# Handing a block's repeated dt x input to the drives when it is loaded

## The chip, the cores and the metric

The kernel runs on one core of one Trainium2 chip. The core has five engines that work side by side, each through its own queue and strictly in the order of that queue: PE (matrix products), DVE (vector), ACT (activations), POOL (a second, slower vector engine) and SP, which here only issues DMAs. The metric is device time of one execution in microseconds, as the median of several runs: 3704.53 us before the change (three runs, 3703.52 to 3707.54).

## The reference

Two layers on a batch of 8 images with 384 channels and 32 x 32 pixels, all in float32. The first is a state-space (Mamba-like) layer, the second a small mixture of experts; the part that the change touches is the scan of the first:

```python
dt = softplus(dt @ dt_proj_w.T + dt_proj_b)
dA  = exp(einsum('bld,dn->bldn', dt, A))            # "decay"
dBu = einsum('bld,bln->bldn', dt * xc, Bm)          # "drive"
h   = dA_t * h + dBu_t                              # scan over the 1024 tokens
y_t = einsum('bdn,bn->bd', h, C_t)                  # "read" and sum over the 16 states
y   = (y + xc * D) * silu(z)                        # "finish"
t   = gelu((y @ out_proj_w.T) @ mlp_w1.T + b1) @ mlp_w2.T + b2
```

Before it come a group norm, a layer norm, a projection and a short convolution that make xc, z, dt, B and C. After it every expert's `relu(x @ w1 + b1)` is computed for every token, and the four results are weighted by a routing that depends on the whole batch: its second product can only start when all tokens have been scored.

## The kernel before, in words

The 8 x 1024 tokens are cut into 16 chunks of 512 tokens. A chunk has 768 inner channels with 16 states each. These are worked off in **rounds**: 6 blocks of 128 channels, and for each block 4 rounds, so 24 rounds a chunk and 384 in all. One round holds 128 channels x 4 states; a tile row holds one of 32 channels and one of 4 states, and four such tiles make the round: two of pair A, two of pair B. So dt and dt x input must stand in SBUF with each channel repeated on four partitions. `delta` (L464) makes them for a block: it computes dt, multiplies it with the input (POOL, `dtx` L489), writes both to DRAM and reads them back with repetition: `dtr_a` and `dtr_b` (dt for the decays of pair A and B) and `dxr` (dt x input, four loads of 256 KB). `dxr` and `dtr_b` have two buffers, `dtr_a` has one.

A round then goes through the engines like this:

- ACT: four decays (L854), two of pair A and two of pair B, into three PSUM buffers.
- POOL: the **drive** (L866), one multiplication of `dxr` by the row of B, 128x2048, into one of five `du` buffers. The buffer comes free when PE has summed the round that used it five rounds ago.
- DVE: four scans (L874), and for pair A the read-outs (L878), products with the row of C.
- POOL: the **read** of pair B (L878, 128x1024), after the pair's scans; in the even chunks a carry copy (L883) before it.
- PE: for every two rounds 16 small products (`y`, L901) that sum over the states. They wait for the reads of both rounds.
- After a block's last sum DVE multiplies with z (`finish`, L911). When all six blocks of a chunk are finished, PE may start that chunk's out projection (L554), and then its MLP (L576, L618); later the experts' first products (L729) of the chunk.

PE, ACT and DVE do the chunk's projections, norms and MLP between the rounds. The order in every queue is written by a planner that is part of the kernel and runs when it is built. It holds a clock of its own for PE, DVE, ACT and POOL, with a fixed duration for each kind of step, and at each moment issues on a free engine the due step of the earliest round, or a side task that fits before the next one. Two of its chains matter here, both on POOL: `pool_a` holds the 384 drives and `pool_b` the 384 reads. A drive is due when the planner has issued the sums that free its buffer and when `dxr` of its block is on the planner's list. If a drive and a read are due at once, the one of the earlier round goes first. What is issued goes into the engine's queue in that order; the real waits are set by semaphores on the data.

A block's `dxr` gets onto that list in `delta`, in this passage (L519 to L529):

```python
        x4 = pdt.tile([P, Q, T], F32, name="dxr")
        for j in range(Q):
            repeat(x4[:, j, :], there_x, j)
            yield "-", PIECE / 2 if i + d else 0
        while issued["A"] < last:
            yield "-", POLL
        dxr[i, d] = x4
```

`last` is the last round of the block before. `issued["A"]` is the last round whose pair A decays the planner has put into ACT's queue. So the planner lets no drive of a block go before the last pair A decay of the block before it is issued. That wait is needed for `dtr_a`, which has a single buffer and is loaded in the lines that follow; `dxr` has a second one.

After the scans (some 3022 us in) PE does the last chunk's out projection and MLP, the routing is worked out, the experts' remaining first products follow, and then only the experts' second products (L1235). Half of chunk 13's expert products and all of the last two chunks' are held back by the kernel until the last chunk is summed.

Of the kernel before, what the change touches and what calls it, by code (L numbers as in the profile page):

```python
# [49 lines left out]
DMA = 3.5  # L50
# [27 lines left out]
def build(tc, io):  # L78
# [3 lines left out]
    with ExitStack() as outer:  # L82
# [47 lines left out]
        with ExitStack() as ctx:  # L130
            layers(ctx, tc, io, ident, cmean, eps, dram, x1_dram, gn1, logits, r_dram, group_norm)


def layers(ctx, tc, io, ident, cmean, eps, dram, x1_dram, gn1, logits, r_dram, group_norm):
# [83 lines left out]
    xc, zs, dtr, dxr, dbc, bc_dram, bt, ct, gn = {}, {}, {}, {}, {}, {}, {}, {}, {}  # L218
# [13 lines left out]
    def bank(name):  # L232
        held[0] += 1
        current[0].holds += 1
        return ps_g.tile([P, T], F32, name=name, tag="g")

    def free():
        held[0] -= 1
        current[0].holds -= 1
# [214 lines left out]
    def written(name, i, d, what):  # L454
        there = dram.tile([P, T], F32, name=f"{name}_dram{i}_{d}")
        nc.sync.dma_start(there, what)
        return there

    def repeat(into, there, j):

        rows = there[j * (P // Q):(j + 1) * (P // Q), :]
        nc.sync.dma_start(into, rows.unsqueeze(1).to_broadcast([P // Q, Q, T]))

    def delta(i, d):  # L464
        while i not in dbc or making_dt:
            yield "-", POLL
        making_dt.append((i, d))
        yield "bank", MM
        g = bank("g_dt")
        PE.matmul(g, lhsT=w_dt[:, d * P:(d + 1) * P], rhs=dbc[i], start=True, stop=True)  # L470
        yield "ACT", EVICT_ROW
        projected.add((i, d))
        dt = p1.tile([P, T], F32, name="dt")
        S.activation(dt, g, AF.Relu, bias=b16[:, d:d + 1], scale=-1.0)
        yield "ACT", 0.7
        S.activation(dt, dt, AF.Exp, bias=top, scale=-1.0)
        yield "ACT", FUNC
        S.activation(dt, dt, AF.Ln, bias=1.0)
        yield "DVE", TAIL
        V.scalar_tensor_tensor(dt, g, b_dt[:, d:d + 1], dt, ALU.add, ALU.max)  # L480
        yield "-", 0
        free()
        there = written("dtr", i, d, dt)
        if i + d == 0:
            yield "DVE", JOIN
        else:
            yield "POOL", MULT
        dtx = p1.tile([P, T], F32, name="dtx")
        (G if i + d else V).tensor_tensor(dtx, dt, xc[i, d], ALU.mult)  # L489
        yield "-", 0  # L490
        there_x = written("dxr", i, d, dtx)
        yield "-", DMA if i + d else 0
        making_dt.clear()
        if i + d == 0:

            b, a = pdt.tile([P, 2, T], F32, name="dtr_b"), p1.tile([P, 2, T], F32, name="dtr_a")
            x4 = pdt.tile([P, Q, T], F32, name="dxr")
            repeat(b[:, 0, :], there, 2)
            for j in (2, 3):
                repeat(x4[:, j, :], there_x, j)  # L500
            repeat(a[:, 0, :], there, 0)
            for j in (0, 1):
                repeat(x4[:, j, :], there_x, j)
            repeat(b[:, 1, :], there, 3)
            repeat(a[:, 1, :], there, 1)
            dtr[i, d], dxr[i, d] = {"A": a, "B": b}, x4
            return
        last = i * per + d * NG - 1
        while issued["B"] < last - NG:
            yield "-", POLL  # L510
        dtr[i, d] = {}
        pair = pdt.tile([P, 2, T], F32, name="dtr_b")
        for k in range(2):
            repeat(pair[:, k, :], there, 2 + k)
        yield "-", 0
        while issued["drive"] < last - NG:
            yield "-", POLL
        dtr[i, d]["B"] = pair
        x4 = pdt.tile([P, Q, T], F32, name="dxr")  # L519
        for j in range(Q):  # L520
            repeat(x4[:, j, :], there_x, j)
            yield "-", PIECE / 2 if i + d else 0
        while issued["A"] < last:
            yield "-", POLL
        dxr[i, d] = x4
        pair = p1.tile([P, 2, T], F32, name="dtr_a")
        for k in range(2):
            repeat(pair[:, k, :], there, k)
        dtr[i, d]["A"] = pair  # L529


    stats = {}
    tt, x1, hs, pre, ready = {}, {}, {}, {}, {}
# [426 lines left out]
    def begin(*new, rank=2, after=None, holds=0):  # L960
        for t in new:
            tasks.append(Task(t, rank, now[0] if after is None else after))
            tasks[-1].holds += holds
# [96 lines left out]
    def plan(i, k):  # L1060

        n = i + 1
        if k % 4 == 1 and k // 4 + 2 < ND:
            begin(delta(i, k // 4 + 2), rank=0)
        if k in (2, 3, 4):
            begin(gate(i, k + 1))
        if k == 4:
            begin(silus(zs, gates, [(i, d) for d in range(3, 6)]))
        if n < NCH:
            if 4 <= k < 10:  # L1070
                begin(conv(n, k - 4), rank=1)
            if k in (6, 9):
                begin(silus(xc, accs, [(n, k - 6 + d) for d in range(3)]), rank=1)
            if k in (11, 12, 13):
                begin(gate(n, k - 11))
            if k == 9:
                begin(x_proj(n), rank=1)
            if k == 13:
                begin(silus(zs, gates, [(n, d) for d in range(3)]))
            if k == 15:  # L1080
                begin(delta(n, 0), rank=0)
            if k == 20:
                begin(delta(n, 1), rank=0)
        if k == 20 and n + 1 < NCH:
            begin(norm(n + 1), rank=1)
        if k == 3 and i + NH < NCH:
            begin(next_x(i))
        if k == 3 and i % NH == 0 and i + NH < NCH:
            begin(statistics(i // NH + 1), rank=3)
# [248 lines left out]
```

## Time and profile before

One execution was profiled: 3700.98 us, with a span of 3699.2 us from the first to the last instruction.

| | |
|---|---|
| median of three runs | 3704.53 us |
| the profiled execution | 3700.98 us |
| its span | 3699.2 us |
| PE busy | 3483.4 us, 94% |
| DVE busy | 3071.8 us, 83% |
| POOL busy | 2771.7 us, 75% |
| ACT busy | 2352.6 us, 64% |
| 383 drives on POOL (L866) | 1737.4 us, 4.542 us each |
| 384 reads on POOL (L878) | 906.4 us, 2.362 us each |
| mean granted PE clock | 0.971 of full speed |

The shares are means over stages that differ. Until some 65 us the first chunk is normalized and projected; then the rounds run, from the first drive at 67 us to the last sum at 3024 us; after that DVE, ACT and POOL have little to do. The tables of busy time by stretches of time, in the next section, show this better than the shares of the whole.

### The profile page before, as it was taken

Reading aid. Unit: us, or ns where it says so; the run is one execution under the profiler, and the core shown is the slowest. Engines: PE = TensorE matmul, PEld = TensorE weight load, DVE = VectorE, ACT = ScalarE, POOL = GpSimd, SP = SyncE. Lnnn points to the kernel's source line nnn. Section 1 sums busy time; section 2 is a strip of 40 time slices with the busy share of each in tenths; the row PEclk is TensorE's granted clock in tenths of the full one; section 3 lists DMA queues with packets and bytes.
Section 4 is the critical chain, followed back from the end, with each engine's and each line's share of the span. In section 5 each row is a group of like instructions: output and inputs, shape, how many; then the busy total and the mean of one; then the engine's idle time right before and its main releaser. Section 6 shows DMA issues by size and latency. Waiting matters only on the chain.

```text
span 3699.2 us, 35905 instructions
## 1 busy us (share of the span) xinstructions
PE 3483.4 (94%) x10342; PEld 1406.0 (38%) x10342; DVE 3071.8 (83%) x3675; ACT 2352.6 (64%) x3714; POOL 2771.7 (75%) x1071
## 2 busy tenths in 40 slices
PE   6759797999999999999999999999999999999999
PEld 3213232334333433333333333333433334444444
DVE  4999999899999999999999999999999861355554
ACT  4758687868787878786978787879687743100000
POOL 2999999899999999999899999998999960000000
PEclk8869898999999999999999999999999999999999
DMA  3434455465656565656565656565655544655552
GB/s 121 152 125 154 157 175 191 161 207 184 201 176 215 187 211 181 201 191 216 176 214 182 215 178 207 191 211 180 211 167 204 187 145 145 228 187 186 187 187 101
DMA packets 387928, 674.81 MB, mean 182 GB/s; under 512 B 42876, under 2 KB 153852, under 8 KB 385556
## 3 DMA queue, kind: packets, MB, share of 16 engines
q1 hardware_dynamic: 385568, 672.18, 54.5%
q8 instruction: 84, 1.38, 0.2%
q14 instruction: 112, 0.92, 0.1%
q10 hardware_dynamic: 2164, 0.34, 0.1%
HBM read 534.33 MB, written 138.02 MB: 182 GB/s over the span
## 4 chain that ended last, share of the span: by engine, by line
PE 56%; DVE 20%; ACT 10%; POOL 5%; DMA 4%; issue 4%; SPq 1%; ACTq 0%; POOLq 0%; DVEq 0%
PE acc L1235 13%; PE g_in L342 9%; PE hid L576 8%; DVE da_A L874 7%; PE e_hid L729 7%; DVE du L874 6%; PE acc L618 6%; PE y L901 5%; PE g_out L554 5%; POOL du L866 3%; DVE du L878 3%; POOL du L878 2%; ACT da_B L854 1%; PE g_dt L470 1%; ACT L222 1%
## 5 line engine op out<-in xcount | busy, mean ns | idle before, releaser
L866 POOL TENSOR_TENSOR du<-dxr,b 128x2048 f32<-128x2048 f32 x383 | 1737.4, 4542 | 0.8 <-DMA b<-bc_dram 0.8
L878 POOL TENSOR_TENSOR du<-du,c 128x1024 f32<-128x1024 f32 x384 | 906.4, 2362 | 109.5 <-DVE du L874 88.6
L854 ACT ACTIVATE da_A<-dtr_a,w_a_log 128x512 f32<-128x512 f32 x768 | 519.8, 686 | 235.4 <-DVE du L878 68.0
L854 ACT ACTIVATE da_B<-dtr_b,w_a_log 128x512 f32<-128x512 f32 x768 | 523.0, 686 | 210.3 <-DVE du L878 73.6
L342 PE MATMUL g_in<-xt,in_proj 128*128 128x512 f32 x1152 | 532.8, 604 | 24.1 <-DMA in_proj<-in_in_proj 13.6
L618 PE MATMUL acc<-h,mlp_w 128*128 128x512 f32 x1152 | 535.3, 604 | 20.8 <-ACT h L592 13.1
L878 DVE TENSOR_TENSOR du<-da_A,c 128x512 f32<-128x512 f32 x768 | 529.4, 689 | 24.0 <-DMA c<-bc_dram 0.2
L576 PE MATMUL hid<-tt,mlp_w 128*128 128x512 f32 x1152 | 520.9, 597 | 6.9 <-DMA mlp_w<-in_mlp_w 1.6
L874 DVE TENSOR_TENSOR_SCAN da_A<-da_A,carry,du 128x512 f32<-128x512 f32 x384 | 490.7, 1278 | 23.0 <-POOL du L866 14.3
L874 DVE TENSOR_TENSOR_SCAN du<-da_B,carry,du 128x512 f32<-128x512 f32 x384 | 475.8, 1269 | 35.4 <-ACT da_B L854 35.0
L1235 PE MATMUL acc<-r,w_e_w 128*128 128x512 f32 x1152 | 494.6, 592 | 0.0
L729 PE MATMUL e_hid<-xn,e_w 128*128 128x512 f32 x1008 | 464.1, 601 | 22.2 <-DMA e_w<-in_e_w 11.3
L874 DVE TENSOR_TENSOR_SCAN da_A<-da_A,du 128x512 f32<-128x512 f32 x384 | 467.3, 1217 | 19.0 <-POOL du L866 12.9
L901 PE MATMUL y<-du,sel 128*32 128x512 f32 x3072 | 413.1, 623 | 69.5 <-POOL du L878 56.7
L874 DVE TENSOR_TENSOR_SCAN du<-da_B,du 128x512 f32<-128x512 f32 x384 | 452.8, 1207 | 26.9 <-ACT da_B L854 25.8
L342 PEld LDWEIGHTS g_in<-xt,in_proj 128*128 128x128 f32 x1152 | 218.6, 193 | 318.7 <-issue 266.4
L618 PEld LDWEIGHTS acc<-h,mlp_w 128*128 128x128 f32 x1152 | 216.7, 192 | 315.1 <-issue 256.9
L576 PEld LDWEIGHTS hid<-tt,mlp_w 128*128 128x128 f32 x1152 | 214.1, 190 | 298.0 <-issue 246.2
L1235 PEld LDWEIGHTS acc<-r,w_e_w 128*128 128x128 f32 x1152 | 218.9, 190 | 275.5 <-issue 275.3
L729 PEld LDWEIGHTS e_hid<-xn,e_w 128*128 128x128 f32 x1008 | 190.0, 192 | 272.0 <-issue 223.3
L554 PE MATMUL g_out<-xc,out_proj 128*128 128x512 f32 x576 | 265.2, 601 | 0.0
L743 ACT ACTIVATE r<-e_hid,w_e_b 128x512 f32<-128x512 f32 x192 | 129.5, 679 | 153.4 <-PE e_hid L729 90.7
(135 smaller groups left out, 3049.0 us busy)
## 6 DMA issues: line engine op xcount, KB each, us to landing
dxr<-dxr_dram SPq DMA_DIRECT2D x384, 256.0 KB, 4.6
mlp_w<-in_mlp_w SPq DMA_DIRECT2D x384, 192.0 KB, 3.6
dtr_b<-dtr_dram SPq DMA_DIRECT2D x192, 256.0 KB, 3.3
dtr_a<-dtr_dram SPq DMA_DIRECT2D x192, 256.0 KB, 3.1
r_dram<-r SPq DMA_DIRECT2D x192, 256.0 KB, 3.8
r<-r_dram SPq DMA_DIRECT2D x64, 768.0 KB, 4.6
in_proj<-in_in_proj SPq DMA_DIRECT2D x192, 192.0 KB, 3.9
e_w<-in_e_w SPq DMA_DIRECT2D x192, 192.0 KB, 4.1
```

The lines of the kernel that those rows point to most:

```text
L342: PE.matmul(g, lhsT=w[:, j, :], rhs=xt[i][:, j, :], start=(j == 0), stop=(j == J - 1))
L554: PE.matmul(g, lhsT=w[:, d, :], rhs=xc[i, 3 * k + d], start=(k + d == 0), stop=(k == 1 and d == 2))
L576: PE.matmul(g, lhsT=w[:, j, :], rhs=tt[i][:, j, :], start=(j == 0), stop=(j == J - 1))
L618: PE.matmul(g, lhsT=w[:, n, :], rhs=hs[mine[n]], start=(k + n == 0), stop=(k == 1 and n == 2))
L729: PE.matmul(h, lhsT=w[:, j, :], rhs=xn[:, j, :], start=(j == 0), stop=(j == J - 1))
L743: S.activation(r, h, AF.Relu, bias=e_b1[:, u:u + 1])
L854: S.activation(da[r, j], dtr[i, d][pair][:, j % 2, :], AF.Exp, scale=neg_a[:, d, j, s:s + 1])
L866: G.tensor_tensor(du[r], dxr[i, d], wide(bt[i, s].unsqueeze(1), [P, Q, T]), ALU.mult)
L874: V.tensor_tensor_scan(a if j < 2 else b, a, b, start, ALU.mult, ALU.add)
L878: engine.tensor_tensor(du[r][:, js, :], h, wide(ct[i, s].unsqueeze(1), [P, js.stop - js.start, T]), ALU.mult)
L901: PE.matmul(y[j * m:(j + 1) * m, :], lhsT=sel, rhs=h[:, j, :], start=False, stop=(s == NG - 1), tile_position=(0, j * m), skip_group_check ...
L1235: PE.matmul(acc[j], lhsT=e2[:, e, d, j, :], rhs=r[:, d, :], start=(e + d == 0), stop=(e + d == E + J - 2))
```

## The change

The assignment that puts `dxr` on the planner's list no longer stands behind the wait for the pair A decays. It goes into a small task that waits for the planner's DMA time (3.5 us on the planner's clock) and then makes the assignment. The load of `dtr_a` still waits.

```diff
         for j in range(Q):
             repeat(x4[:, j, :], there_x, j)
             yield "-", PIECE / 2 if i + d else 0
+        begin(repeated(i, d, x4), rank=0)
         while issued["A"] < last:
             yield "-", POLL
-        dxr[i, d] = x4
         pair = p1.tile([P, 2, T], F32, name="dtr_a")
         for k in range(2):
             repeat(pair[:, k, :], there, k)
         dtr[i, d]["A"] = pair
 
+
+    def repeated(i, d, x4):
+        yield "-", DMA
+        dxr[i, d] = x4
```

Both kernels hold the same instructions, kind by kind and shape by shape, on all five engines. What differs is the order in which they stand in the queues.

## The prediction

> **What bounds the kernel now.** I read the busy time by stages first, because the page's shares mix them. This table of stretches has, for each engine, busy time and number of instructions, then the granted PE clock:
>
> ```profile
> core 0: us, PE busy (x) PEld busy (x) DVE busy (x) ACT busy (x) POOL busy (x), PEclk, DMA share, GB/s
> 0.00:150.00 150.00, 101.38 (x278) 42.75 (x278) 95.62 (x130) 87.93 (x151) 80.24 (x48) 0.83 0.45 141
> 150.00:640.00 490.00, 396.52 (x1188) 143.20 (x1188) 465.13 (x566) 353.27 (x554) 464.96 (x186) 0.87 0.48 156
> 640.00:2850.00 2210.00, 2159.97 (x6791) 862.62 (x6790) 2066.63 (x2470) 1735.46 (x2739) 2063.29 (x788) 0.99 0.59 195
> 2850.00:3022.00 172.00, 165.59 (x536) 65.88 (x534) 157.75 (x163) 121.04 (x187) 162.49 (x51) 1.00 0.56 187
> 3022.00:3199.20 177.20, 165.18 (x400) 72.84 (x401) 24.73 (x51) 53.61 (x82) 0.73 (x2) 0.97 0.43 142
> ```
>
> PE is the bound over the whole: the products are a fixed amount of work, and the span is that work plus PE's idle time. In the long stage (640 to 2850) PE idles for 50.0 us of 2210. Before 640 it idles for 93.5 us of 490: there it runs out of work and waits for the scans, and DVE (95%) and POOL (95%) set the pace. So an earlier scan is worth something before 640 and next to nothing from there to 2850.
>
> Who waits in that first stage, 150 to 640 (in all, times, longest); one answer per engine, DVE, POOL and PE:
>
> ```profile
> DVE da_A L874 <- POOL du L866: 8.0, 9, 2.0
> DVE du L874 <- ACT da_B L854: 4.1, 7, 1.3
> ...
> POOL du L878 <- DVE du L874: 11.6, 8, 4.9
> POOL carry L883 <- DVE du L874: 10.1, 5, 5.0
> ...
> PE y L901 <- POOL du L878: 50.8, 13, 9.1
> ```
>
> DVE waits 8.0 us for drives; POOL waits 21.7 us with a read at the head of its queue whose scans are not done; PE waits 50.8 us for reads. A queue that puts a drive where POOL now waits would shorten the first two together. The end of the first chunk in POOL's timeline shows the opposite price:
>
> ```profile
> 247.45 2.35 POOL L878 TENSOR_TENSOR du<-du,c 128x1024 f32<-128x1024 f32 x1
> 249.75 9.01 POOL L866 TENSOR_TENSOR du<-dxr,b 128x2048 f32<-128x2048 f32 x2
> 258.70 0.19 POOL L883 COPY carry<-du 128x2 f32<-128x2 f32 x1
> 258.98 2.34 POOL L878 TENSOR_TENSOR du<-du,c 128x1024 f32<-128x1024 f32 x1
> ```
>
> The chunk's last read (round 23) stands behind two drives of later rounds, and the chain then goes on through PE's out projection at 263 us. A drive ahead of a read costs that read up to 4.54 us.
>
> Last the end of the scans, in PE's timeline:
>
> ```profile
> 3019.28 1.91 PE L901 MATMUL y<-du,sel 128*32 128x512 f32 x12
> 3022.58 1.05 PE L901 MATMUL y<-du,sel 128*32 128x512 f32 x4 [1.39 <-POOL du L878]
> 3023.56 15.72 PE L554 MATMUL g_out<-xc,out_proj 128*128 128x512 f32 x36
> ```
>
> PE waits only 1.39 us for the last read: its work and the scans end together, so from here a later scan costs its full length.
>
> **What the change moves.** No instruction is added or removed, no DMA either; a drive moves ahead of reads in POOL's queue, and the other queues shift a little with the planner's clock. Counting in the built order how many rounds' reads are still open when a drive is queued: before 145 drives stand one ahead, 234 two, 1 three; after 38, 249 and 93. The first difference is at round 12, some 165 us in.
>
> *Step 1, 150 to 640 us.* In the new order a drive stands in front of the read for which POOL waited 3.2 us at 172 us, and one drive fewer stands ahead of the read of round 23 (25 drives against 26, so 4.54 us less POOL work before it); ahead of round 47's there is one more (51 against 50), ahead of round 71's the same number. So at the third chunk's end, 627 us, POOL has the same work behind it, and its gain is what it no longer waits: at most 21.7 us. DVE has no less to do either and can gain at most its waits for drives, 8.0 us; its other waits (ACT, PE) stay. Both have to move, so I take the smaller, -8.0 us, all of it on the path since PE is out of work there. Ends: -21.7 us (POOL's whole waits, if DVE's other waits shrink too) and +4.5 us (the extra drive before round 47 and nothing gained).
>
> *Step 2, 640 to 2850 us.* DVE waits 16.6 us more for drives, but PE's queue sets the pace and its waits for reads are 1.7 us in 850 to 2850: gain 0 to -2 us. Against it: with more drives ahead, the read that completes a pair has on average 2.8 us more POOL work before it over all pairs, while the sums stand after 6.2 us less PE work in pairs 150 to 185 (both by counting the orders with the page's mean durations, a big product at 0.92 us). That is 8.0 us by which PE comes nearer to the reads there. Before, the sums end in the median 3.8 us after the pair's read, of which 1.9 us are the sums themselves, so 1.9 us are slack. The shift is an offset that is paid once, not per round, since POOL idles 146.7 us in this stage and can catch up: 0 to +6.1 us. I take 0, for POOL's 6.6% idle is the nearest row and it is larger than the offset.
>
> *Step 3, drives that wait for a buffer.* An odd round's drive needs the sums of the pair five and four rounds back. 31 odd drives now stand three ahead, right behind the read that completes that pair, so POOL would wait up to 3.8 us (the row above) each, 118 us at most, where it now never waits for PE. Taken at 0, hidden in the 146.7 us; without this cover PE would see the 3.8 us less its 1.9 us of slack, 31 times, +59 us.
>
> *Step 4, DMA.* The four `dxr` loads are issued at least 12.0 us (median 21.5) before the block's first drive and land in 4.6 us, 7.0 at most. A drive that is earlier by one or two drives still finds them there: 0, with the 7.0 us of one landing as the upper end. SP's queue holds the same issues; `dtr_a` still waits for the last decay.
>
> *Step 5, the end.* Two expert units (six products, 5.5 us by 0.46 us a record) that stood before the last sum now stand behind it. They fill idle time if the scans end earlier, and PE also idles 12.0 us after 3022, so 0; +5.5 us if neither holds.
>
> Sum: -8.0 us against the profiled execution's own 3700.98, that is 3693.0. The profiled execution lies 3.55 us under the median of the runs, so on the scale of the runs 3704.5 - 8.0 = 3696.5 us.
>
> **Two rules of the Trainium skill.** POOL's timeline above shows the read of round 23 held for 9.01 us by two drives that it does not need. "PSUM — Partial Sum Buffer", Engine vs sequencer instructions, says why: "ScalarE/VectorE/GpSimdE queues are strict FIFO". By that rule alone every read with a drive newly in front pays 4.54 us, and step 1 would be +4.5; the trace's POOL waits of 21.7 us say that part of it falls into time in which the read could not have run.
>
> The granted clock in 190 to 230 us is 0.57 and in 425 to 450 us 0.66, where PE waits 3.7, 5.1 and 4.6 us for reads. "TensorE: Matmul & The Clock Gate", What's actually happening, has the array drop to half rate after an idle window of about 3.4 us. By that rule shorter waits would also speed up the products between them: 11.64 us of PE work in 425 to 450 us would become 7.7 at full clock, an estimate of 4 us more. The sum leaves it out, because PE waits for the scans again right after.
>
> **The rivals.**
>
> *The gain is eaten at a chunk's end (no change).* Round 23 comes earlier, but PE only runs dry earlier before round 47, which has one more drive ahead. For it: PE has no other work from 425 to 450 us (busy 11.64 of 25). Against it: from 330 to 416 us POOL waits 11.2 us for scans, room for two drives. Time: -8.0 + 4.5 = -3.5 us, 3701.0.
>
> *The read-outs come late (slower).* Place: PE's queue from pair 150 on, where sums stand 8.0 us nearer to their reads and in the last seven pairs 14.0 us. Price: 8.0 - 1.9 = +6.1 to 14.0 - 1.9 = +12.1 us, and nothing of step 1 reaches the end: about +10, 3714.5. It decides once a read is more than its 1.9 us of slack late; step 3's waits push the same way. For it: at 3022 us PE and scans end together. Against it: POOL's idle time in the long stage.
>
> *The change does nothing.* Excluded for the order (93 drives three ahead); for the time it is the first rival.
>
> **How the numbers follow.** Forecast (-8 us and around it, down to -20): 0.42. No change to speak of: 0.25. Later reads, in the forms of steps 2, 3 and 5: 0.33, because three separate steps have an upper end that costs and the whole order of five queues shifts. About 0.2%, 7.4 us, is what a measurement of this kernel can tell from no change; -8.0 lies just past it. The range goes from -20.5 us (step 1's lower end nearly whole) 3684 to +17.5 us (rival two with step 5's 5.5) 3722; the forecast's own range is 3684 to 3698.
>
> **What would show it.** In the profile after: DVE's waits for drives in 150 to 640 us near zero and POOL's for scans clearly under 21.7; out projections of chunks 0 to 2 earlier than 263, 448 and 641 us, by 5, 3 and 8 us; PE idle in that stage under 93.5. If instead a new wait of POOL's drives for PE appears, or PE's waits for reads in 850 to 2850 grow from 1.7 us to ten or more, the second rival holds. The prediction is wrong if the third chunk's end is earlier and the end is not.

## The result and the profile after

The changed kernel takes 3717.24 us (median of 8 runs, 3710.68 to 3720.32) against 3705.06 us (8 runs, 3701.12 to 3707.54) for the kernel before: ratio 1.0034, 95% interval 1.0024 to 1.0043. It is 12 us slower; the forecast was 8 us faster. The profiled execution took 3716.37 us with a span of 3714.6 us, 15.4 us more than before.

The stretches of time of the changed kernel, with the columns of the table shown of before (busy time of each engine and its instructions, then the granted PE clock):

```profile
core 0: us, PE busy (x) PEld busy (x) DVE busy (x) ACT busy (x) POOL busy (x), PEclk, DMA share, GB/s
150.00:640.00 490.00, 396.26 (x1206) 141.76 (x1210) 463.74 (x566) 352.24 (x554) 470.55 (x187) 0.88 0.49 157
640.00:2850.00 2210.00, 2147.75 (x6734) 857.39 (x6727) 2055.93 (x2459) 1732.74 (x2732) 2051.26 (x782) 0.99 0.59 193
```

In the first stage PE has 18 more records (1206 against 1188), but no more work: it is busy for 396.3 us against 396.5, and its idle time there, 93.7 us against 93.5, did not fall. In the long stage it did 57 records fewer (6734 against 6791) and idled 62.3 us instead of 50.0. Over the whole span PE idles 10.4 us more (226.2 against 215.8) and its products take 5.0 us longer (3488.4 against 3483.4); together these are the 15.4 us.

The waits of that first stage, DVE's, POOL's and PE's, as they were shown of before:

```profile
DVE du L878 <- ACT da_B L858: 5.7, 8, 2.0
DVE da_A L878 <- ACT da_A L858: 5.4, 6, 1.7
DVE da_A L878 <- POOL du L870: 4.2, 4, 2.0
...
POOL du L882 <- DVE du L878: 7.2, 6, 3.9
POOL du L870 <- PE y L905: 3.4, 2, 2.4
POOL carry L887 <- DVE du L878: 3.0, 5, 1.5
...
PE y L905 <- POOL du L882: 61.3, 19, 8.3
```

POOL's waits for scans fell from 21.7 to 10.2 us and DVE's for drives from 8.0 to 4.2. DVE's two waits for decays rose from 6.3 to 11.1 us; of these the one for pair A was, before:

```profile
DVE da_A L874 <- ACT da_A L854: 2.2, 2, 1.5
```

POOL's timeline around the last read of the first chunk shows what was predicted of it: before, two drives (249.75 to 258.76 us) stood right ahead of that read; now one does, and the two come behind it.

```profile
245.00 4.51 POOL L870 TENSOR_TENSOR du<-dxr,b 128x2048 f32<-128x2048 f32 x1
249.45 0.19 POOL L887 COPY carry<-du 128x2 f32<-128x2 f32 x1
249.72 2.36 POOL L882 TENSOR_TENSOR du<-du,c 128x1024 f32<-128x1024 f32 x1
252.05 9.02 POOL L870 TENSOR_TENSOR du<-dxr,b 128x2048 f32<-128x2048 f32 x2
```

That read ends at 252.1 us, before at 261.3; the third chunk's last read ends at 620.2 instead of 626.9. How that came about is seen in the busy time from 150 us to this read, first before, then after (columns as above):

```profile
150.00:626.90 476.90, 383.42 (x1158) 138.16 (x1158) 452.19 (x552) 344.34 (x540) 451.86 (x182) 0.87 0.47 154
150.00:620.20 470.20, 377.30 (x1142) 134.69 (x1142) 446.71 (x549) 338.92 (x532) 451.64 (x181) 0.88 0.49 156
```

POOL has done the same work by then and idled 6.5 us less. DVE has idled only 1.2 us less and done 5.5 us less work: three instructions now come after the read. PE has idled 0.6 us less and done 6.1 us less work. So for PE and DVE most of the gain at this point is work that comes later.

Over the whole span, these are four waits of the changed kernel, three of them new or grown and the last one shorter:

```profile
ACT da_A L858 <- DMA dtr_a<-dtr_dram: 68.7, 25, 9.1
DVE da_A L878 <- ACT da_A L858: 43.6, 36, 3.9
POOL du L870 <- PE y L905: 33.1, 20, 5.6
DVE da_A L878 <- POOL du L870: 9.7, 12, 2.0
```

In the kernel before they read:

```profile
ACT da_A L854 <- DMA dtr_a<-dtr_dram: 32.4, 14, 10.1
DVE da_A L874 <- POOL du L866: 27.2, 40, 2.0
DVE da_A L874 <- ACT da_A L854: 13.6, 15, 2.2
```

DVE's waits for drives went from 27.2 to 9.7 us, and its waits for pair A's decays from 13.6 to 43.6: one wait took the other's place. ACT waits for the reload of pair A's dt, which follows the last decay of the block before; POOL's drives now wait for the sums that free their buffer.

The end of the scans in PE's timeline:

```profile
3030.21 1.92 PE L905 MATMUL y<-du,sel 128*32 128x512 f32 x16
3032.07 2.84 PE L733 MATMUL e_hid<-xn,e_w 128*128 128x512 f32 x6
3034.74 2.74 PE L558 MATMUL g_out<-xc,out_proj 128*128 128x512 f32 x6
3037.32 2.74 PE L733 MATMUL e_hid<-xn,e_w 128*128 128x512 f32 x6
3039.89 13.04 PE L558 MATMUL g_out<-xc,out_proj 128*128 128x512 f32 x30
```

The last sum ends 8.5 us later than before (3032.1 against 3023.6). Of the two expert units that moved behind it one stands right behind it and one within the out projection, and the time from there to the first of the last products (L1235, here L1239) is 182.8 us instead of 175.8. The shifts add up: -6.7 us at the third chunk's last read, +13.7 from there to the last chunk's last read, +1.5 from that read to the last sum, and +7.0 behind it.

### The profile page after: what moved, and what is told of

Its sections match the earlier page's. It is cut to its first block, busy times and chain, and to the rows that moved or that the text cites. A ratio compares the mean times of both kernels' runs of the same rounds, so it can differ in the third digit from the quotient of the medians.

```text
span 3714.6 us, 35879 instructions
## 1 busy us (share of the span) xinstructions
PE 3488.4 (94%) x10342; PEld 1406.5 (38%) x10342; DVE 3068.4 (83%) x3675; ACT 2355.0 (63%) x3714; POOL 2773.2 (75%) x1071
## 4 chain that ended last, share of the span: by engine, by line
PE 56%; DVE 19%; ACT 10%; POOL 5%; DMA 5%; issue 4%; SPq 1%; ACTq 0%; POOLq 0%; DVEq 0%
PE acc L1239 13%; PE e_hid L733 9%; PE hid L580 7%; PE g_in L342 7%; DVE da_A L878 7%; PE acc L622 7%; DVE du L878 6%; PE y L905 5%; PE g_out L558 4%; POOL du L870 4%; DVE du L882 4%; ACT L222 1%; ACT da_B L858 1%; POOL du L882 1%; ACT da_A L858 1%
## 5 line engine op out<-in xcount | busy, mean ns | idle before, releaser
L870 POOL TENSOR_TENSOR du<-dxr,b 128x2048 f32<-128x2048 f32 x383 | 1735.0, 4539 | 33.9 <-PE y L905 33.1
L733 PE MATMUL e_hid<-xn,e_w 128*128 128x512 f32 x1008 | 472.3, 610 | 31.9 <-DMA e_w<-in_e_w 16.6
L1239 PE MATMUL acc<-r,w_e_w 128*128 128x512 f32 x1152 | 494.6, 592 | 0.0
L1239 PEld LDWEIGHTS acc<-r,w_e_w 128*128 128x128 f32 x1152 | 218.9, 190 | 275.5 <-issue 275.3
```

The lines of the kernel that those rows point to most:

```text
L733: PE.matmul(h, lhsT=w[:, j, :], rhs=xn[:, j, :], start=(j == 0), stop=(j == J - 1))
L870: G.tensor_tensor(du[r], dxr[i, d], wide(bt[i, s].unsqueeze(1), [P, Q, T]), ALU.mult)
L1239: PE.matmul(acc[j], lhsT=e2[:, e, d, j, :], rhs=r[:, d, :], start=(e + d == 0), stop=(e + d == E + J - 2))
```

## The experiments

Three theories stood at the beginning. A: the loss is the reload of pair A's dt, which has one buffer and was hidden behind the first drive of a block. B: it is the drives that wait for their buffer's sums and hold the reads behind them. C: it is neither, but what any new order of the five queues does to the time. Later two more names come up: D, that the change itself costs and the kernel before has an ordinary order; E, that the drives' place in POOL's queue is what costs.

### The change in part of the chunks

```diff
+        if i < 3:                                 # second run: i >= 3
             begin(repeated(i, d, x4), rank=0)
         while issued["A"] < last:
             yield "-", POLL
+        if not (i < 3):
+            dxr[i, d] = x4
```

> The early hand-over only in chunks 0 to 2, the old condition from chunk 3 on. Theory A (the loss is made in the long stage, because pair A's dt tile has one buffer and its reload is no longer covered by the first drive) and theory B (drives queued too far ahead wait for their buffer's sums and hold the reads behind them): the start keeps its gain, third chunk's end about 7 us earlier than before, no new wait in the long stage; 0 to 7 us faster than before, about 3701. Theory C (the loss is only the scatter of a newly laid order of all queues): anywhere within 12 us of before on either side, with no tie to the two waits.

Measured: 3695.54 us, ratio 0.9978 (0.9969 to 0.9987). The third chunk's last read ends at 619.1 us, 7.8 earlier than before, the last sum 6.7 earlier, and by the ratio 8 us (5 to 11) arrive at the end. ACT's wait for the reload is 41.2 us. By the two traces all five queues hold the same instructions in the same order as in the kernel before from 953 us on (but for two pairs of neighbouring PE records), so this run shows the early start with the rest as it was.

> The early hand-over only from chunk 3 on. Theories A and B: the whole loss and none of the gain, 12 to 20 us slower than before (3717 to 3725), ACT's wait for the reload of pair A's dt near 60 us and POOL's wait of drives for sums near 30 us. Theory C: no tie, within 12 us of before on either side.

Measured: 3688.23 us, ratio 0.9958 (0.9944 to 0.9971), faster where A and B said 12 to 20 us slower. And it is faster with their waits in place:

```profile
ACT da_A L861 <- DMA dtr_a<-dtr_dram: 55.1, 21, 9.9
DVE da_A L881 <- ACT da_A L861: 35.4, 29, 3.4
POOL du L873 <- PE y L908: 21.3, 15, 3.1
```

So the two visible waits can't be what makes the changed kernel slow, at least not by themselves. The gains of the two parts (-8 and -16 us by the ratios) don't add up to the whole (+12 us) either.

### The planner knows when pair A's dt lands

```diff
             repeat(pair[:, k, :], there, k)
+        yield "-", DMA
         dtr[i, d]["A"] = pair
```

> The changed kernel, but the planner hands pair A's dt to the decays only a DMA time (3.5 us) after issuing its load, so that it puts other work of ACT into the reload instead of queueing a decay that has to wait. Theory A: ACT's wait for that load falls from 68.7 us to under 30, DVE's wait for pair A decays from 43.6 to under 20, and 8 to 14 us of the time come back (3703 to 3709). Theory B: the waits of ACT may fall, POOL's 33 us for sums stay, and the time stays within 4 us of the changed kernel's 3717. Theory C: some change without order.

Measured: 3679.11 us, ratio 0.9937 (0.9925 to 0.995), 38 us under the changed kernel. But ACT's wait for the reload is still 64.0 us, DVE's for pair A's decays 40.9 and POOL's for sums 26.1. The time came back, and far more than A allowed, while the waits that were to give it stayed. The edit did something else: it laid another order.

### Drives one buffer less ahead

```diff
-            pool_a += [Step(go, "POOL", DRIVE, [summed_with(r - DUS)] if r >= DUS else [], drive_of,
+            pool_a += [Step(go, "POOL", DRIVE, [summed_with(r - DUS + 1)] if r >= DUS else [], drive_of,
```

> The changed kernel, but a drive is due only when the sums of the round four back (not five) are planned, so no drive is queued as far ahead. Theory B: POOL's wait of drives for sums falls from 33 us to near 0 and 8 to 14 us of the time come back (3703 to 3709). Theory A: that wait goes, but ACT's wait for the reload of pair A's dt stays above 50 us and the time stays within 4 us of 3717. Theory C: some change without order.

Measured: 3750.04 us, ratio 1.013 (1.0115 to 1.0145). POOL's wait for sums is gone, ACT's for the reload down to 22.0 us, and it is 33 us slower than the changed kernel: DVE now waits 56.8 us for drives and PE 87.3 us for reads. Against B: its wait went and the time rose. This edit lays a new order as well, though, so how much of the 33 us comes from the later drives is not shown.

### What another number of the planner does

Four numbers of the planner were moved a little, each in both kernels. None is the duration of a drive, a read or a decay. Two of them are used in `delta`, though: 1.23 us is the planner's time for the product that makes dt x input, and the polling step also times the wait for the pair A decays. Nothing that is computed changes; the order of the queues is laid anew.

```diff
-LAG = 0.04
+LAG = 0.05                                        # p1
-DRIVE, READ_B, MULT = 4.49, 2.32, 1.23
+DRIVE, READ_B, MULT = 4.49, 2.32, 1.27            # p2
-POLL = 0.5
+POLL = 0.4                                        # p3
-TAP_1, TAP_2, JOIN, TAIL, STATS, GATED = 0.77, 0.67, 0.72, 0.64, 0.60, 0.59
+TAP_1, TAP_2, JOIN, TAIL, STATS, GATED = 0.77, 0.67, 0.72, 0.64, 0.60, 0.66   # p4
```

> The kernel before, with one number of the planner moved that has nothing to do with drives or pair A (its lag between two engines, 0.04 to 0.05 us). It lays the order of all queues anew. Theory C (scatter of the order): the time moves by 3 to 15 us to either side of before. Theory D (the kernel before has an ordinary order, and the change itself costs): it stays within 4 us of before.

> The changed kernel with the same number moved (lag 0.04 to 0.05 us). Theory C: it moves by 5 to 25 us against the changed kernel's 3717, and its difference to its partner without the change can have either sign. Theory D: it is 8 to 16 us slower than its partner.

> The kernel before, with the planner's duration of the dt x input product moved from 1.23 to 1.27 us (1.26 in the trace). Theory C: 3 to 15 us to either side of before. Theory D: within 4 us of before.

> The changed kernel with the same number moved (1.23 to 1.27 us). Theory C: 5 to 25 us off the changed kernel's 3717, either sign against its partner. Theory D: 8 to 16 us slower than its partner.

> The kernel before, with the planner's polling step moved from 0.5 to 0.4 us. Theory C: 3 to 15 us to either side of before. Theory D: within 4 us of before.

> The changed kernel with the same number moved (0.5 to 0.4 us). Theory C: 5 to 25 us off the changed kernel's 3717, either sign against its partner. Theory D: 8 to 16 us slower than its partner.

> The kernel before, with the planner's duration of the finishing product moved from 0.59 to 0.66 us (0.67 in the trace). Theory C: 3 to 15 us to either side of before. Theory D: within 4 us of before.

> The changed kernel with the same number moved (0.59 to 0.66 us). Theory C: 5 to 25 us off the changed kernel's 3717, either sign against its partner. Theory D: 8 to 16 us slower than its partner.

Measured, as ratio to the kernel before with its interval. The last four columns are the ends of the last read of chunks 0, 2, 3 and 15 in the profiled execution, from POOL's timeline:

| number moved | kernel | ratio | interval | chunk 0 | chunk 2 | chunk 3 | chunk 15 |
|---|---|---|---|---|---|---|---|
| none | old | 1 | | 261.3 | 626.9 | 809.0 | 3022.5 |
| lag | old | 1.0036 | 1.0022 to 1.0050 | 262.1 | 626.3 | 810.9 | 3039.6 |
| product | old | 1.0075 | 1.0060 to 1.0090 | 263.2 | 629.6 | 816.0 | 3053.1 |
| polling | old | 1.0025 | 1.0016 to 1.0035 | 256.7 | 627.4 | 813.5 | 3031.0 |
| finish | old | 1.0083 | 1.0066 to 1.0100 | 254.9 | 630.0 | 815.9 | 3061.0 |
| none | new | 1.0034 | 1.0024 to 1.0043 | 252.1 | 620.2 | 808.1 | 3029.5 |
| lag | new | 1.0025 | 1.0016 to 1.0034 | 251.9 | 617.3 | 804.8 | 3023.9 |
| product | new | 1.0003 | 0.9993 to 1.0012 | 254.9 | 623.9 | 807.8 | 3022.3 |
| polling | new | 1.0059 | 1.0044 to 1.0074 | 252.8 | 620.6 | 805.6 | 3047.8 |
| finish | new | 0.9932 | 0.9917 to 0.9947 | 253.9 | 618.2 | 804.2 | 2988.8 |

This settles most of it. Moving one of these numbers costs the old kernel 0.25% to 0.83%, and moves the new one from -0.68% to +0.59% of before. The change's own +0.34% lies inside that spread. New against old, pair by pair: +0.34%, -0.11%, -0.72%, +0.34%, -1.51%, on average -0.33%; with a scatter of 0.79% over five pairs the 95% interval of that mean is some 1% to either side, so the sign of the change's effect on the whole time is not settled. Theory D falls: three of the pairs don't have the new kernel 8 to 16 us slower.

The columns say where the scatter comes from. At the third chunk's end the five old orders lie between 626.3 and 630.0 us, mean 628.0, and the five new ones between 617.3 and 623.9, mean 620.0: the new ones are all earlier, by 8.0 us on average. The time from there to the last read, the long stage, is 2395.6 to 2431.0 us in the old orders (mean 2413.4, scatter 14) and 2370.6 to 2427.2 in the new ones (mean 2402.4, scatter 21). The unchanged kernel has the shortest long stage of its five and is the fastest of them. On PE itself the start's gain is smaller than 8 us: its idle time in 150 to 640 us is 98.3 us on average in the old orders and 92.4 in the new ones, but 93.5 and 93.7 in the pair in which no number is moved. So an earlier start is there on average, and the long stage hides it under an order that happens to be some tens of microseconds longer or shorter.

### The other queues held

To separate the drives' place in POOL's queue from the new order of all others, the change was made by hand. In the first two runs the planner runs exactly as in the kernel before, and PE, DVE, ACT and SP have the same queues row for row; only when a read is put into POOL's queue may the next drive be put in ahead of it.

```diff
+        loaded[i, d] = x4, now[0] + DMA            # in delta, after the loads
...
             def read_b(r=r):
+                n = emitted[0] + 1
+                if n < rounds:
+                    i, d, s = at(n)
+                    if (s == 0 and n >= DUS and n - r <= 3          # second run: n >= DUS and n - r <= 2
+                            and summed_with(n - DUS) in ends and (i, s) in bt
+                            and loaded.get((i, d), (0, 1e9))[1] <= now[0]):
+                        ahead.add(n)
+                        emit_drive(n, loaded[i, d][0])
```

> All queues but POOL's in exactly the order of the kernel before; in POOL's queue alone the first drive of a block moves ahead of reads as soon as its data and buffer allow, up to three rounds ahead (69 drives stand three ahead, 202 two, 109 one). This is the change without the new order of the other queues. Theory E (the drives' place on POOL is what costs): 8 to 16 us slower than before, with POOL's wait of drives for sums near 30 us. Theory C (the new order of the other queues is what costs): within 5 us of before, or up to 8 us faster by the shorter start.

Measured: 3751.87 us, ratio 1.0135 (1.0119 to 1.0152), 49 us slower than before with four queues unchanged. POOL's drives wait for sums only 1.7 us, so it is not B. What has grown is PE's wait for reads, here with the kernel before's first line and this run's second:

```profile
PE y L901 <- POOL du L878: 56.7, 16, 9.1
```

```profile
PE y L908 <- POOL du L885: 102.8, 41, 8.3
POOL du L885 <- DVE du L881: 105.1, 49, 4.7
POOL carry L890 <- DVE du L881: 81.7, 47, 4.7
```

PE's idle time over the span (span less busy) went from 215.8 to 236.9 us, and its products took 25 us longer (busy 3508.5 against 3483.4). A block's first drive three rounds ahead puts 4.54 us in front of a read that PE's queue expects where it was. POOL then waits 186.8 us for scans instead of 151.2: having spent the drive early, it has none to put into those waits.

> As the kernel before in all queues but POOL's, and there every drive stands two rounds ahead of the reads wherever its data and buffer allow (379 of 380). Theory E: 10 to 25 us slower than before, since all reads with a drive newly in front are later. Theory C: within 5 us of before, or up to 8 us faster.

Measured: 3695.84 us, ratio 0.9981 (0.9972 to 0.9991), 7 us faster than before. With an even lead of two, DVE's waits for drives drop out of its longest waits and ACT's for the reload is 17.8 us. So with everything else held the same idea gives -0.19% in one form and +1.35% in another; theory E holds for the drives that go three ahead out of step with the other queues, and not for the lead as such.

The third run goes the other way: the changed kernel's four queues held, and its 93 drives that stand three ahead put behind the next read.

```diff
         issued["drive"] = r
-        du[r] = pdu.tile([P, Q, T], F32, name="du")
+        if r > 4 and r - reads_done[0] >= 3:
+            held_back.append(r)
+        else:
+            emit_drive(r)
...
+                reads_done[0] = r + 1              # in read_b, after the read
+                emit_held()
...
```

> All queues but POOL's in exactly the order of the changed kernel; in POOL's queue the 93 drives that stand three ahead are put behind the next read (342 two ahead, 38 one), as they nearly stand before the change. Theory E: POOL's wait of drives for sums goes and 8 to 14 us come back (3703 to 3709). Theory C: the wait goes, but the time stays within 5 us of the changed kernel's 3717.

Measured: 3731.76 us, ratio 1.0075 (1.0062 to 1.0088), 14.5 us slower than the changed kernel. POOL's wait for sums fell from 33.1 to 12.9 us as intended, and ACT's for the reload rose to 86.4. Neither theory had that. Taking away 20 us of the buffer wait, the changed kernel's newest line, brought no time back. That its drives stand well where its other queues expect them is argued from this, not shown.

### Two buffers for pair A's dt

A second buffer takes 4 KB more of every partition. Seven hidden tiles of the MLP instead of nine make room for it. The first run is the partner with one buffer; both have the same order in all five queues.

```diff
-HID = 9
+HID = 7                                            # both runs
...
-            b, a = pdt.tile([P, 2, T], F32, name="dtr_b"), p1.tile([P, 2, T], F32, name="dtr_a")
+            b, a = pdt.tile([P, 2, T], F32, name="dtr_b"), pdt.tile([P, 2, T], F32, name="dtr_a")   # second run
...
-        pair = p1.tile([P, 2, T], F32, name="dtr_a")
+        pair = pdt.tile([P, 2, T], F32, name="dtr_a")   # second run
```

> The changed kernel with seven instead of nine hidden tiles of the MLP, which frees the room for the next run. It is only that run's partner: the planner lays another order and holds hidden products back, so its time may lie anywhere from 3690 to 3790; ACT's wait for the reload of pair A's dt stays at 40 to 80 us.

Measured: 3698.05 us, ratio 0.9991 (0.9982 to 1.0000).

> As its partner with seven hidden tiles, every queue in the same order, but pair A's dt has two buffers, so that its reload need not wait for the last decay of the block before. Theory A (the exposed reload is what costs): ACT's wait for the reload falls under 10 us and the time by 10 us or more against the partner. Theory C (the order decides, and this wait falls into time that ACT and DVE have anyway): the wait falls as much, but the time stays within 5 us of the partner's.

Measured: 3692.90 us, ratio 0.9974 (0.9965 to 0.9983), 5 us under the partner. The expected wait did not go. ACT's two lines, the partner's first:

```profile
ACT da_A L858 <- DMA dtr_a<-dtr_dram: 48.7, 24, 10.1
```

```profile
ACT da_A L858 <- DMA dtr_a<-dtr_dram: 54.6, 23, 10.4
```

What went is the wait of SP's queue, where the load of pair A's dt stood until ACT had read the old one:

```profile
SPq L462 <- ACT da_A L858: 158.3, 72, 11.6
```

```profile
SPq L462 <- ACT da_A L858: 1.1, 2, 0.8
```

The load still stands at the same place in SP's queue, right behind the point at which the planner has issued the last decay, and the decays of the next block are queued on ACT as if it landed at once; so ACT waits for the landing, not for the buffer. Of theory A about 5 us are shown, for this order: the buffer's share. The landing's share wasn't isolated.

### Both edits that came out fast

> Knowing the landing of pair A's dt (as in the run with that one edit) together with the finishing product's duration of 0.66 us, against the changed kernel with 0.66 alone (0.9932 of before). If knowing the landing helps in itself, as it seemed by 1% on the changed kernel, this is again 15 to 38 us faster than that partner (3642 to 3665). Theory C: it has either sign against the partner, most likely slower, since that partner was the fastest of its row.

Measured: 3675.31 us, ratio 0.9927 (0.9914 to 0.9939), 4.5 us under its partner of 3679.81 (the intervals of the two overlap) and not 15 to 38. So most of the 38 us that the knowledge of the landing seemed to be worth on the changed kernel was the order it laid. It has the lowest median of this study, 0.7% under the kernel before. It keeps the change, and PE gets through more records in the long stage than before (6842 against 6791):

```profile
640.00:2850.00 2210.00, 2170.67 (x6842) 867.80 (x6840) 2091.62 (x2501) 1753.27 (x2770) 2089.89 (x796) 1.00 0.60 197
```

## Why the prediction was wrong

*Step 1, the first 640 us, -8.0 us: near in the number, in part by luck.* The third chunk ends 6.7 us earlier in the changed kernel, 7.8 with the change in three chunks alone, and 8.0 on average over five orders of each kind. POOL's half held: the same work and 6.5 us less idle time. DVE's half did not: its waits for drives fell by 3.8 us, its waits for decays, which were to stay, rose by 4.8, and it came to the chunk's end earlier because 5.5 us of its work were put behind that end. Of the signs, the out projections start 8.0, 1.8 and 2.4 us earlier (forecast 5, 3 and 8; the third starts at 632.3 us before, not at 641), and PE's idle time in the stage did not fall (93.7 against 93.5).

*"All of it on the path": right only where the rest stays as it was.* With the change in three chunks alone the gain of 8 us arrived at the end. With the whole change 0.9 us of it are left at the fourth chunk's end; over the five orders of each kind 7.0 are left there on average.

*Step 2, the long stage, "I take 0": this is the step that failed.* The changed kernel's long stage is 13.7 us longer (2409.3 against 2395.6, chunk 2's last read to chunk 15's). The prediction priced the offset of reads against sums, 0 to +6.1 us, and took the rest of the order as if it stayed. It does not: a new place for 93 drives moves the planner's clock, and with it thousands of steps. What such a new order costs by itself, 14 to 21 us of scatter in this stage, was the largest term and stood nowhere in the sum, and the unchanged kernel was at the short end of it. Over the five orders of each kind the long stage is 11.0 us shorter with the change on average, less than the scatter, so a cost of the change itself in this stage is not shown. PE's waits for reads, which were to tell, stayed at 1.4 us in 850 to 2850 (1.7 before). PE waited instead for weights, 24.3 us against 9.5 in 640 to 2850. The changed kernel's lines, which read 5.3, 1.6 and 2.6 us before, are:

```profile
PE e_hid L733 <- DMA e_w<-in_e_w: 10.8, 5, 3.9
PE hid L580 <- DMA mlp_w<-in_mlp_w: 7.7, 3, 2.7
PE acc L622 <- DMA mlp_w<-in_mlp_w: 5.8, 2, 4.2
```

That is as large as the loss, but the version that knows the landing has the same waits (24.8 us) and is 23 us faster than before. Which of the changed kernel's rows makes its long stage long is not settled.

*Step 3, drives that wait for a buffer, taken at 0: the wait came (33.1 us of at most 118), a price was not seen.* Taking 20 us of it away with the other queues held brought no time back.

*Step 4, DMA for the drives, 0: right.* No drive waits for `dxr` except the first of all. The reload of pair A's dt, which the moved line used to give time, was named only as unchanged; it is the wait that took the drives' place (DVE 43.6 us against 13.6), and this should have been a rival.

*Step 5, the two expert units, taken at 0: its upper end was right.* The tail is 7.0 us longer; over the five orders of each kind it is 4.2 us longer on average. Two units are 5.5 us, and they did not fill PE's idle time from 3022 us on: it is 16.4 us against 17.3.

*The rivals.* "The read-outs come late" came near in time, 3714.5, but not in the cause: it named PE's queue from pair 150 on, and PE's waits for reads didn't grow in the long stage. As a mechanism it exists: in the run with four queues held, 49 us slower, PE's waits for reads grew by 46 us. PE's idle time grew by only 21 us there, and why its products took 25 us longer is open. "The gain is eaten at a chunk's end" had the place right: the 9.2 us gained at the first chunk's last read are 1.7 at the second's (442.2 against 443.9 us); but 6.7 are there again at the third's.

*The two rules.* By "PSUM — Partial Sum Buffer" of the Trainium skill, Engine vs sequencer instructions, POOL's queue is strictly first in, first out, so that a read waits for every drive queued in front of it. The run with a block's first drive three ahead agrees: PE's waits for reads went from 56.7 to 102.8 us. With an even lead of two they are 64.3 us, and the kernel is 7 us faster all the same. By "TensorE: Matmul & The Clock Gate", What's actually happening, the array drops to half rate after an idle window of about 3.4 us. The products would then go faster where long waits are fewer, and the runs don't settle that: PE was busy for 3508.5 us in the run with most waits for reads and for 3469.8 in the fastest version, at mean granted clocks of 0.969 and 0.972, but the changed kernel has 0.969 as well and 3488.4 us.

## What to carry to other kernels

Where a planner writes all queues, a change at one point lays a new order everywhere, and the price of a new order has to be known first: move two or three other numbers and see how far the time goes. A change smaller than that scatter can't be judged by one run of the whole, only by holding the other queues fixed, by the stage where it acts, or over several orders of each kind. And when a wait is removed from a plan, look for what else it covered: here the reload of a tile with a single buffer.

## What the runs showed that was not expected

Moving a planner's duration closer to its measured value made the old kernel slower both times (1.23 to 1.27 us where the trace has 1.27: +0.75%; 0.59 to 0.66 us where it has 0.68: +0.83%), and the second made the new one faster (-0.68% of before). Identical instructions in other orders took from 0.9927 to 1.0135 of the time before; with four of the five queues as before, from 0.9981 to 1.0135. PE's busy time, for the same 10342 products, ranged from 3469.8 to 3508.5 us over these versions.
